# Projections on four column groups of TensorE in place of the whole array, in a two-layer attention kernel

## The chip, the cores and the metric

The kernel runs on one core of a Trainium2 chip. The metric is the device time of one execution in microseconds (us); the median of several runs is quoted, with the lowest and highest in brackets. The work is bound by TensorE, the matrix engine, an array of 128 rows (the contracted dimension, partitions of the two inputs) by 128 columns (partitions of the output). A matmul can use the whole array (written 128\*128 below), four groups of 32 rows (32\*128, four small contractions side by side) or four groups of 32 columns (128\*32, four narrow outputs side by side).

A **wave** below is four matmuls, one for each group, that run at once. A **pass** is one matmul record of the trace: a matmul of f32 stands there as two records, so as two passes. A **set** is the four matmuls that take the place of one full-width matmul, so two waves. A **hand-over** is the distance between the start of the last matmul of one shape and the first of the next.

## The reference

Eight images of 32 x 32 positions and 512 channels go through two layers; each adds an attention over the group-normalised input. Cut to what matters:

```
# layer 0: 16 heads of 32 channels, N = 1024 positions
qkv = gn(x) @ w_qkv                          # 3 projections 512 -> 512
attn = softmax(q * 32**-0.5 @ k^T)           # per head, 1024 x 1024
x = x + (attn @ v) @ w_proj + b_proj         # 1 projection

# layer 1: 4 heads of 128 channels, with relative position logits
q, k, v = gn(x) @ Wq, gn(x) @ Wk, gn(x) @ Wv # 3 projections
scores = q @ k + position_logits(q)          # small matmuls with pos_emb_w, pos_emb_h
x = x + (softmax(scores) @ v) @ Wo           # 1 projection
```

That is eight projections an image, everything in f32.

## The kernel before

The first attention is a chain of 64 steps an image. A step has scores in four row groups, `exp` on ScalarE (ACT), and the product with v in four column groups. Its sums of `exp` are made by VectorE (DVE) and finished by a small matmul in four column groups:

```python
# attention_0, front: scores, 32*128
for r in range(HB):                       # HB = 4
    nc.tensor.matmul(ps[:, r, :], k[m][rows, j*P:(j+1)*P], q[m][rows, h*NB:(h+1)*NB], start=True, stop=True)
nc.scalar.activation(e, ps, AF.Exp, scale=D0 ** -0.5)    # ps has one buffer
# back: product with v, 128*32
    nc.tensor.matmul(acc[r*D0:(r+1)*D0, :], v[:, j, c0:c0+D0], e[:, r, :], start=(j == 0), stop=(j == NT-1))
nc.vector.tensor_add(state["esum"], state["esum"], e)
# finish, after eight steps: su = sum of esum, 128*32; then reciprocal on VectorE
```

`ps` has one buffer, so the next scores can't start before `exp` has read the last ones. Into the time in which TensorE would wait for `exp`, the kernel weaves the other work of the neighbouring images, above all the projections. There are three helpers, all with the same loop; a bank of PSUM gets four matmuls over the contracted chunks `cc`, so eight passes:

```python
def project_T(xn, w, dsts, name):
    for m in range(CC):
        for h in range(NH):
            pa = bank(f"pa_{name}_{m}_{h}")
            for cc in range(CC):                  # CC = 4
                nc.tensor.matmul(pa, w[:, cc, m*P:(m+1)*P], xn[cc][:, h*NB:(h+1)*NB],
                                 start=(cc == 0), stop=(cc == CC - 1))
            evacuate(dsts(m)[:, h*NB:(h+1)*NB], pa)       # copy on ScalarE
            yield CC
# project_rows and product_T: the same loop
```

The argument will come to the position logits as well. Their matmuls are in column groups of 32, and each result is written as a rounded number by ScalarE and a rest by VectorE, one needing the other:

```python
nc.scalar.copy(view[rows], pp[rows, :, i])                                      # "posT", ACT CAST
nc.vector.tensor_sub(view[rests], pp[rows, :, i], view[rows].bitcast(F32))      # "posT", DVE
```

## Time and profile before

| | before |
|---|---|
| median of 3 runs | 4286.79 us (4285.86 to 4296.93) |
| profiled execution, span | 4285.4 us |
| TensorE (PE) busy | 97% |
| VectorE, ScalarE busy | 54%, 39% |
| idle of TensorE ahead of the first attention's scores | 49.6 us, of which 49.2 ended by `exp` |
| share of TensorE in the chain that ended last | 85% |

Busy time is the union of an engine's instructions over the span. An engine at 97% that also carries the chain is the bound: what is taken off it comes off the time, unless what comes next was waiting for another engine. The lines are shown and read in the prediction.

### The profile page before, as it was taken

What the parts mean: (1) busy time and instruction counts of PE and PEld (TensorE: products, weight loads), DVE (VectorE), ACT (ScalarE), POOL (GpSimd) and SP (SyncE); (2) the same over time, 40 slices, a digit from 0 to 9 for tenths busy, and PEclk for the clock granted to TensorE, in tenths of its full rate; (3) what the DMA queues carried; (4) which work ended last, traced back from release to release, by engine and by line L of the source; (5) the groups of instructions that cost most, each with busy time, mean ns of one, the idle gap of its engine ahead of it and who ended that gap; (6) DMA issues with size and microseconds to landing.
All of it is one profiled execution on the core that took longest, in us unless ns stands there. A gap on an engine that the chain in (4) does not pass through costs nothing.

```text
span 4285.4 us, 42293 instructions
## 1 busy us (share of the span) xinstructions
PE 4167.0 (97%) x17602; PEld 1577.6 (37%) x17602; DVE 2313.8 (54%) x2105; ACT 1673.2 (39%) x1793; POOL 247.9 (6%) x155
## 2 busy tenths in 40 slices
PE   7999999999999999999999999999999999999998
PEld 3222333333333333333333333333333333333443
DVE  2565466354663547635576355663556635467334
ACT  1553444324443244432444324443244333444131
POOL 0000000000010000100000000000000000000000
PEclk9999999999999999999999999999999999999999
DMA  4101110131101311012110121102210022010201
GB/s 118 35 20 45 30 40 1 40 89 30 40 1 40 89 30 40 1 54 74 33 37 1 69 59 42 28 1 74 58 41 15 1 74 55 30 40 1 84 15 21
DMA packets 320808, 170.66 MB, mean 40 GB/s; under 512 B 271424, under 2 KB 271456, under 8 KB 320608
## 3 DMA queue, kind: packets, MB, share of 16 engines
q1 hardware_dynamic: 320512, 167.81, 13.7%
q8 instruction: 140, 2.29, 0.2%
q14 instruction: 60, 0.49, 0.0%
q0 software_dynamic: 96, 0.07, 0.0%
HBM read 117.51 MB, written 50.33 MB: 39 GB/s over the span
## 4 chain that ended last, share of the span: by engine, by line
PE 85%; DVE 8%; ACT 4%; issue 1%; DMA 0%; POOL 0%; SPq 0%; DVEq 0%; ACTq 0%; POOLq 0%
PE ps L270 11%; PE pa_q L208 11%; PE pp L456 10%; PE ps L379 10%; PE acc L289 10%; PE pa_v L223 10%; PE acc L391 9%; PE pa_k L208 7%; DVE rc L256 3%; PE ps L380 2%; ACT e L278 2%; DVE posT L366 2%; DVE es L300 2%; ACT posT L365 2%; PE su L309 1%
## 5 line engine op out<-in xcount | busy, mean ns | idle before, releaser
L300 DVE TENSOR_TENSOR es<-es,e 128x2048 f32<-128x2048 f32 x384 | 889.5, 2316 | 919.2 <-ACT e L278 918.9
L278 ACT ACTIVATE e<-ps 128x2048 f32<-128x2048 f32 x512 | 961.7, 1878 | 838.1 <-PE ps L270 724.1
L270 PE MATMUL ps<-q,k 32*128 32x512 f32 x4096 | 609.5, 644 | 49.6 <-ACT e L278 49.2
L256 DVE RECIPROCAL rc<-su 128x512 f32<-128x512 f32 x128 | 429.3, 3355 | 316.4 <-PE su L309 297.6
L379 PE MATMUL ps<-q,k 128*128 128x512 f32 x1024 | 547.6, 616 | 14.9 <-DVE checks L237 14.3
L289 PE MATMUL acc<-e,v 128*32 128x512 f32 x4096 | 553.2, 611 | 1.0 <-ACT e L278 1.0
L391 PE MATMUL acc<-e,v 128*128 128x512 f32 x1024 | 525.4, 596 | 0.7 <-ACT e L382 0.7
L382 ACT ACTIVATE e<-ps 128x512 f32<-128x512 f32 x512 | 305.1, 597 | 563.5 <-PE ps L380 455.5
L258 POOL TENSOR_TENSOR q<-hd,rc 128x512 f32<-128x512 f32 x128 | 225.8, 1764 | 3506.2 <-DVE rc L256 3288.0
L380 PE MATMUL ps<-posT,sel 128*128 128x512 f32 x512 | 406.9, 795 | 0.0
L402 DVE TENSOR_TENSOR es<-es,e 128x512 f32<-128x512 f32 x384 | 277.0, 721 | 162.6 <-ACT e L382 151.8
L270 PEld LDWEIGHTS ps<-q,k 32*128 32x128 f32 x4096 | 166.3, 184 | 422.1 <-issue 205.7
L379 PEld LDWEIGHTS ps<-q,k 128*128 128x128 f32 x1024 | 174.9, 189 | 338.0 <-issue 259.0
L391 PEld LDWEIGHTS acc<-e,v 128*128 128x128 f32 x1024 | 192.9, 190 | 151.3 <-issue 110.9
L128 ACT COPY q<-pa_q 128x512 f32<-128x512 f32 x128 | 74.9, 585 | 440.1 <-PE pa_q L208 439.8
L208 PE MATMUL pa_q<-x0T,wq 128*128 128x512 f32 x512 | 236.9, 609 | 5.3 <-DMA wq<-in_L_conv_w_qkv 4.6
L223 PE MATMUL pa_v<-wv,x1T 128*128 128x512 f32 x512 | 236.7, 612 | 2.3 <-DVE posT L366 2.3
L366 DVE TENSOR_TENSOR posT<-pp,posT 32x256 fp32r<-32x256 f32 x256 | 130.2, 509 | 196.6 <-ACT posT L365 195.1
L208 PE MATMUL pa_q<-x1T,wq 128*128 128x512 f32 x512 | 232.9, 606 | 3.1 <-DVE x1T L192 3.1
L208 PE MATMUL pa_k<-x0T,wk 128*128 128x512 f32 x512 | 233.7, 602 | 0.0
L223 PE MATMUL pa_v<-wv,x0T 128*128 128x512 f32 x512 | 233.3, 602 | 0.0
L208 PE MATMUL pa_k<-x1T,wk 128*128 128x512 f32 x512 | 232.4, 602 | 0.6
(67 smaller groups left out, 2822.4 us busy)
## 6 DMA issues: line engine op xcount, KB each, us to landing
xs<-in_x SPq DMA_DIRECT2D x128, 128.0 KB, 3.1
d<-x0T SPq DMA_DIRECT2D x32, 512.0 KB, 3.7
x1T<-d SPq DMA_DIRECT2D x32, 512.0 KB, 5.9
d<-x1T SPq DMA_DIRECT2D x32, 512.0 KB, 2.6
x2T<-d SPq DMA_DIRECT2D x32, 512.0 KB, 6.7
out<-ot SPq DMA_DIRECT2D x256, 64.0 KB, 1.9
wq<-in_L_conv_w_qkv SPq DMA_DIRECT2D x8, 1024.0 KB, 7.7
wk<-in_L_conv_w_qkv SPq DMA_DIRECT2D x8, 1024.0 KB, 6.0
```

The source lines that it names most:

```text
L208: nc.tensor.matmul(pa, w[:, cc, m * P : (m + 1) * P], xn[cc][:, h * NB : (h + 1) * NB], start=(cc == 0), stop=(cc == CC - 1),)
L223: nc.tensor.matmul(pa, xn[cc][:, t * P : (t + 1) * P], w[:, cc, :], start=(cc == 0), stop=(cc == CC - 1),)
L256: nc.vector.reciprocal(rec, su)
L270: nc.tensor.matmul(ps[:, r, :], k[m][rows, j * P : (j + 1) * P], q[m][rows, h * NB : (h + 1) * NB], start=True, stop=True,)
L278: nc.scalar.activation(e, ps, AF.Exp, scale=D0 ** -0.5)
L289: nc.tensor.matmul(acc[r * D0 : (r + 1) * D0, :], v[:, j, c0 : c0 + D0], e[:, r, :], start=(j == 0), stop=(j == NT - 1),)
L300: nc.vector.tensor_add(state["esum"], state["esum"], e)
L379: nc.tensor.matmul(ps, k[h][:, keys], q[:, h, queries], start=True, stop=False)
L380: nc.tensor.matmul(ps, sel[:, keys], posT[h][:, queries], start=False, stop=True)
L382: nc.scalar.activation(e, ps, AF.Exp, scale=1.0 / math.sqrt(D1))
L391: nc.tensor.matmul(acc, v[:, j, h * D1 : (h + 1) * D1], e, start=(j == 0), stop=(j == NT - 1),)
L456: nc.tensor.matmul(pa, w[:, cc, m * P : (m + 1) * P], y(cc)[:, h * NB : (h + 1) * NB], start=(cc == 0), stop=(cc == CC - 1),)
```

## The change

The intent: the product with v already runs in four column groups of 32. If the projections run in the same shape, TensorE goes from one to the other without changing shape. The program also holds a general path, which it takes only if its check of the sums of `exp` fails; it is unchanged, and the quick path alone is edited. There the three projection helpers call a new one:

```diff
+    def by_columns(out, weights, moving, start, stop):
+        for g in range(P // 32):
+            columns = slice(32 * g, 32 * g + 32)
+            nc.tensor.matmul(
+                out[columns, :], weights[:, columns], moving, start=start, stop=stop
+            )
 ...
             for cc in range(CC):
-                nc.tensor.matmul(
+                by_columns(
                     pa,
                     w[:, cc, m * P : (m + 1) * P],
                     xn[cc][:, h * NB : (h + 1) * NB],
 ... (the same edit in project_rows and product_T)
```

Each full-width matmul becomes four of 32 columns with the same moving operand. Line numbers in the profile are 8 higher after the change.

More of the change, by code (lines that the diff above doesn't have):

```diff
@@ L222, in project_rows @@
             for cc in range(CC):
-                nc.tensor.matmul(
+                by_columns(
                     pa,
@@ L455, in product_T @@
         for cc in range(CC):
-            nc.tensor.matmul(
+            by_columns(
                 pa,
```

## The prediction

> **What bounds the kernel now.** I read the page's busy shares and the chain that ended last, then the groups, then the timeline of TensorE in stretches small enough to see its hand-overs.
>
> ```profile
> PE 4167.0 (97%) x17602; PEld 1577.6 (37%) x17602; DVE 2313.8 (54%) x2105; ACT 1673.2 (39%) x1793; POOL 247.9 (6%) x155
> ...
> PE 85%; DVE 8%; ACT 4%; issue 1%; DMA 0%; POOL 0%; SPq 0%; DVEq 0%; ACTq 0%; POOLq 0%
> ...
> L270 PE MATMUL ps<-q,k 32*128 32x512 f32 x4096 | 609.5, 644 | 49.6 <-ACT e L278 49.2
> L289 PE MATMUL acc<-e,v 128*32 128x512 f32 x4096 | 553.2, 611 | 1.0 <-ACT e L278 1.0
> L208 PE MATMUL pa_q<-x0T,wq 128*128 128x512 f32 x512 | 236.9, 609 | 5.3 <-DMA wq<-in_L_conv_w_qkv 4.6
> L223 PE MATMUL pa_v<-wv,x0T 128*128 128x512 f32 x512 | 233.3, 602 | 0.0
> ```
>
> TensorE is busy 97% and is 85% of the chain, so a microsecond taken off TensorE is worth nearly a microsecond. The groups name the shape of the array: 32*128 (four row groups) for the first attention's scores, 128*32 (four column groups) for its product with v, 128*128 for the projections. A projection makes 32 matmuls of f32; eight batches of it are 256, and the group says x512: each f32 matmul stands as two records, two passes. There are eight projections a batch, so 8 x 512 = 4096 records, which this change makes 16384.
>
> The pace of a full-width projection is read where nothing else runs:
>
> ```profile
> 82.37 27.63 PE L223 MATMUL pa_v<-wv,x0T 128*128 128x512 f32 x64
> 109.93 1.14 PE L270 MATMUL ps<-q,k 32*128 32x512 f32 x8
> ```
>
> (109.93 - 82.37) / 64 = 0.431 us a pass, hand-over at the end included; in the records of single matmuls the distance is 0.429 us, in 3367 of some 3390 cases. The mean of 602 to 609 ns in the group is a latency: it overlaps the next pass.
>
> A stretch in the steady state, where a step of the first attention is followed by a sum and a projection:
>
> ```profile
> 438.53 1.14 PE L270 MATMUL ps<-q,k 32*128 32x512 f32 x8
> 439.60 1.07 PE L289 MATMUL acc<-e,v 128*32 128x512 f32 x8
> 440.48 1.04 PE L309 MATMUL su<-es,ones 128*32 128x512 f32 x8
> 441.45 3.70 PE L208 MATMUL pa_q<-x1T,wq 128*128 128x512 f32 x8
> 445.08 1.14 PE L270 MATMUL ps<-q,k 32*128 32x512 f32 x8
> ```
>
> Start to start: scores 1.07, product 0.88, sum 0.97, projection 3.63 us. Eight matmuls in four groups are two waves, 2 x 0.429 = 0.858; the projection is 8 x 0.429 = 3.432. What is over is 0.21, 0.02, 0.11 and 0.20. The only hand-over that costs next to nothing is the one from 128*32 to 128*32. And this shows the pace of column groups: the second wave of the product and both of the sum start 0.429 us apart, four matmuls at once in each, the same as one full-width pass.
>
> The weight loads tell the rest:
>
> ```profile
> 438.52 0.31 PEld L270 LDWEIGHTS ps<-q,k 32*128 32x128 f32 x8 [0.76 <-issue]
> 439.60 0.16 PEld L289 LDWEIGHTS acc<-e,v 128*32 128x32 f32 x8 [0.76 <-ACT q L128]
> 440.05 0.13 PEld L309 LDWEIGHTS su<-es,ones 128*32 128x32 f32 x4 [0.30 <-issue]
> 440.48 0.13 PEld L309 LDWEIGHTS su<-es,ones 128*32 128x32 f32 x4 [0.30 <-issue]
> 441.45 0.30 PEld L208 LDWEIGHTS pa_q<-x1T,wq 128*128 128x128 f32 x2 [0.84 <-issue]
> ```
>
> The sum's loads start at 440.05, behind the product's last wave. The projection's first load starts at 441.45, with its matmul, not ahead of it: across a change of shape nothing is loaded ahead. So a change costs twice, once for emptying the array (records: 522 ns instead of 429 between the last and the first start) and once for the first load not hidden: the first pass of a full-width block lasts 533 ns to the second instead of 429, that of a column block 453.
>
> **What the Trainium skill says.** "TensorEngine Tiling (Array Packing)", section Key Properties: a change of tiling mode drains TensorE, a change of tile does not. The trace agrees: 93 ns more. "TensorE: Matmul & The Clock Gate", section Measured speedup vs the span model: tiles start about 4 ns apart and run together. Here they start 7 ns apart, 20 ns from first to fourth. The same page, LDWEIGHTS (loading the stationary operand), gives columns / 1.2 ns, 27 ns for 32 and 107 for 128; the trace has 106 to 110 and 181 to 190, so the trace's are used. The same page, Step-by-step, step 2, gives some 62 ns of decoding a MATMUL where it is done in software; four a wave leave 107 ns each.
>
> **The change part by part.** Arithmetic, moving data and results are the same; each full-width pass of 0.429 us becomes a wave of four column matmuls of 0.429 us. In itself that gains nothing: the work is not small in either direction, so no idle part of the array is filled. Added are 12,288 matmul records and as many loads. What moves are the hand-overs. I sorted the matmul records by start and counted neighbours, by shape:
>
> - Column block to projection: 333, of which 312 at the plain 522 ns (542 from the last wave's first matmul). Each now costs 542 + 533 for the first two passes; as one shape 2 x 429. Saved 217 ns: 312 x 0.217 = 67.7 us.
> - Projection to column block: 45, 43 plain, 32 of them into the position logits (pp). 522 + 453 becomes 858: 117 ns x 43 = 5.0 us.
> - Projection to scores (row groups): 287. The change of shape stays, and must now wait for the fourth group, 20 ns later: -5.7 us.
> - Projection to a full-width block (second attention, group norm): 21, now free, then 217 ns: -4.6 us. The other way round: 9 x 117 ns = -1.1 us.
> - Scores to projection: 7, with 80 ns less first load: +0.6 us.
>
> Sum 61.9 us. Not all of it arrives. In the first batch's stage (113 to 360 us, when there are only projections to fill the gaps) some 15 of 64 steps take 3.1 us and are held by the chain of scores 1.07, exp 1.88 and the next scores; 15 x 0.2 = 3 us don't count. And there, projections were taken in pieces, half a bank at a time: the instruction order made when the program is built may now cut between the four groups of a set, and a cut set costs two waves more, 0.858 us. I put 5 us for that, a guess. Left: 54 us, 1.3%.
>
> **The rivals.**
>
> 1. *The wave is slower than 0.429 us when it lasts.* The trace has at most four waves in a row; a solo projection is 64. Per wave there are eight instructions in 429 ns, 54 ns each. For it: over 50 us TensorE never took more than one per 59 ns so far. Against it: the position logits start 64 matmuls and 64 loads from 459.91 to 461.80 us, 15 ns each, and the densest 20 us have 445 instructions, 45 ns each. If the rate were 62 ns an instruction, a wave would be 0.496 us and 4096 of them 274 us longer: 4560 us. If four streams of the same tile disturbed each other in memory, it would be similar; but the product with v already reads four streams from 128 partitions at 0.429 us.
> 2. *Cut sets.* If the order breaks most of the first stage's 96 sets (24 banks by 4), up to 50 x 0.858 = 43 us are lost and the gain is 15 us: 4270 us.
> 3. *Something else takes over.* DVE 54% and ACT 39% are far from it, and a step with a whole projection has 5.5 us or more against the 3.1 us of scores and exp. The gain should arrive.
> 4. *It is much faster,* as four groups on small work would be. For it speaks only the intent; L289's 4096 records in 553.2 us against L379's 1024 in 547.6 show equal array time for equal work.
>
> **Range and chances.** 4286.8 - 54 gives 4232 us. Without losses it would be 4225; with some unforeseen gain 4210; with cut sets 4270 and a little more for a wave that is some ns slower: 4285. Faster by 2% needs 4201 us, more than all the countable hand-overs: 0.05. Slower by 2% needs 21 ns a wave or more on top: 0.08.
>
> **What would show it.** Right: waves 0.429 us apart in the solo projection before 110 us, which still takes 27.5 us; the hand-over product to projection without the 0.11 us; the projection's loads ahead of it, behind the product's last wave; projection to scores still some 0.11 us; twelve thousand more matmuls but nearly the same busy TensorE. Wrong: waves over 440 ns apart, groups of a set started in different steps, or new idle time of TensorE ended by exp or by the DVE.

## The result, and the profile after

The changed kernel took **4242.48 us** (4241.89 to 4243.49, 4 runs) against 4286.32 us (4283.82 to 4296.93, 4 runs) for the kernel before on the same chip. The ratio is 0.9893, 95% interval 0.9876 to 0.991. Ratios here are the mean time of one kernel's fast runs over that of the other's in the same rounds, so they are not quite the ratio of the quoted medians. The outputs are correct. The profiled executions took 4285.4 us before and 4239.9 us after, 45.5 us apart; all accounts by place below are of these two.

The page of the changed kernel, busy times, chain and TensorE groups (the columns of a group: line, engine, operation, output and inputs, shape, count, then busy us and mean ns, then idle time ahead and what ended it):

```profile
PE 4111.0 (97%) x29890; PEld 1367.7 (32%) x29890; DVE 2314.6 (55%) x2105; ACT 1673.7 (39%) x1793; POOL 248.7 (6%) x155
...
PE 85%; DVE 8%; ACT 4%; issue 1%; DMA 0%; POOL 0%; SPq 0%; DVEq 0%; ACTq 0%; POOLq 0%
...
L278 PE MATMUL ps<-q,k 32*128 32x512 f32 x4096 | 610.1, 645 | 58.4 <-ACT e L286 58.2
...
L297 PE MATMUL acc<-e,v 128*32 128x512 f32 x4096 | 553.3, 611 | 1.0 <-ACT e L286 1.0
...
L206 PE MATMUL pa_q<-x0T,wq 128*32 128x512 f32 x2048 | 237.0, 600 | 5.4 <-DMA wq<-in_L_conv_w_qkv 4.7
```

TensorE has 12,288 more instructions, as counted beforehand, yet is busy 56 us less (4167.0 before); the share in the chain hasn't moved. A projection group is four times as many records in the same busy time (237.0 us; 236.9 before). One number has grown that nothing in the plan should have made grow: the idle time ahead of the scores, 49.6 us before, is 58.4 us.

TensorE's timeline of the changed kernel, start and length in us, at the end of the projections that run alone and at the same steady step that the prediction shows of before:

```profile
82.41 27.65 PE L206 MATMUL pa_v<-wv,x0T 128*32 128x512 f32 x256
110.00 1.14 PE L278 MATMUL ps<-q,k 32*128 32x512 f32 x8
...
437.12 1.07 PE L297 MATMUL acc<-e,v 128*32 128x512 f32 x8
438.00 1.04 PE L317 MATMUL su<-es,ones 128*32 128x512 f32 x8
438.86 3.62 PE L206 MATMUL pa_q<-x1T,wq 128*32 128x512 f32 x32
442.41 1.14 PE L278 MATMUL ps<-q,k 32*128 32x512 f32 x8
```

Alone: (110.00 - 82.41) / 64 = 0.431 us a wave, hand-over included, exactly as a full-width pass before; in the records, waves start 0.429 us apart. Four column groups with the same moving operand are neither faster nor slower than the whole array. In the steady step, sum to projection is 0.86 us in place of 0.97, and projection to scores is 3.55 us in place of 3.63. The weight loads of the same kernel at this place show why:

```profile
438.00 0.13 PEld L317 LDWEIGHTS su<-es,ones 128*32 128x32 f32 x4 [0.30 <-issue]
438.43 0.13 PEld L206 LDWEIGHTS pa_q<-x1T,wq 128*32 128x32 f32 x4 [0.30 <-issue]
```

The projection's first load is at 438.43, a wave ahead of its matmul at 438.86, where before it came with the matmul.

I sorted the matmul records by start and put the distance between neighbours into classes by shape. A distance over 640 ns is split into a plain 520 ns and a wait. Then the account of the 45.5 us is:

| between neighbours | before | after | difference |
|---|---|---|---|
| column block to projection, plain | 172.8 us (333) | 137.4 us (340) | -35.4 |
| within projections, plain | 1644.5 us | 1625.5 us | -19.0 |
| projection to column block, plain | 23.5 us (45) | 19.6 us (51) | -3.9 |
| projection to full width and back, plain | 13.2 us (32) | 16.1 us (32) | +2.9 |
| all others, plain | | | +2.8 |
| waits | 115.3 us | 122.9 us | +7.6 |

The plain parts sum to -52.6 us, and with the waits it is -45.0; the rest of the 45.5 lies ahead of the first matmul and behind the last. Of the +7.6 us of waits, +10.3 are from a projection to the next scores (35.5 to 45.8 us). In some stretches of 3.4 or 6.8 us the profile has TensorE's granted clock at 0.5, and passes of the projections start some 0.85 us apart; what they take longer counts as a wait here. These stretches, the one behind the last work left out, sum to 54.6 us before and 47.8 after. So at most some 3 us of the 45.5 come from this half clock, an estimate: half of the difference.

Where along the run it comes is just as telling. The first scores of the second image start at 361.2 us before and 361.7 us after: the first image's whole stage, from 110 us on, gained nothing. The later images gain 3 to 11 us each; part of that spread is stretches at half clock, which differ from image to image (last section).

**The first stage.** VectorE, ScalarE and TensorE in the changed kernel, a stretch in which a finished sum falls (timeline; the bracket is the idle time ahead of an instruction and what ended it):

```profile
150.34 3.36 DVE L264 RECIPROCAL rc<-su 128x512 f32<-128x512 f32 x1 [1.27 <-PE su L317]
...
154.35 2.92 DVE L306 TENSOR_TENSOR es<-e,e 128x2048 f32<-128x2048 f32 x1
...
157.36 1.88 ACT L286 ACTIVATE e<-ps 128x2048 f32<-128x2048 f32 x1 [3.25 <-DVE es L306]
...
159.29 1.14 PE L278 MATMUL ps<-q,k 32*128 32x512 f32 x8 [0.63 <-ACT e L286]
```

The same stretch before:

```profile
154.64 2.88 DVE L298 TENSOR_TENSOR es<-e,e 128x2048 f32<-128x2048 f32 x1
...
157.62 1.88 ACT L278 ACTIVATE e<-ps 128x2048 f32<-128x2048 f32 x1 [3.00 <-DVE es L298]
159.54 1.14 PE L270 MATMUL ps<-q,k 32*128 32x512 f32 x8
```

Once in eight steps `exp` has to wait for VectorE, which makes reciprocal, check and first sum one after the other (3.36 + 0.69 + 2.92 us), before a buffer for `exp` comes free. Before, TensorE was busy almost long enough to cover it: 157.62 + 1.88 = 159.50, and the scores start at 159.54. The timeline shows no wait, but the records do: 580 ns between the last start of the projection and the first of the scores, in place of 522, so a wait of 0.06 us. After, TensorE is there earlier and waits 0.63 us (1223 ns, so 0.70 us by the records). This is a wait that was almost covered before, and waits of this kind come eight times in the stage: from projections to scores they sum to 0.7 us before and 5.4 after.

The stage has a second loss. In the records, its projections stood in 54 blocks before, mostly of four passes. After, 36 of 55 blocks have four waves, but seven have 14 records, three and a half waves, and seven have only two records: the two passes of one group's matmul, cut off from its set. (A **block** is a run of projection matmuls with no others between them.) The 14 records take 1308 ns from first start to last, four whole waves take 1307: nothing is saved where the matmul was cut off, and where it stands its two passes cost 2 x 0.429 = 0.858 us, as the prediction has it for a cut set. Seven of these are 6 us; four more uneven blocks, of 10, 22, 10 and 6 records, last 16 waves where 12 would do, another 1.7 us. Altogether the blocks of the stage lasted 66.4 us before and 69.2 after, where 54 times the 0.085 us that a four-pass block has become shorter should have saved 4.6.

**The position logits.** A step of the changed kernel while they are written (timeline):

```profile
986.27 1.14 PE L278 MATMUL ps<-q,k 32*128 32x512 f32 x8
...
988.23 3.62 PE L206 MATMUL pa_k<-x1T,wk 128*32 128x512 f32 x32
...
989.79 0.36 ACT L373 CAST posT<-pp 32x256 fp32r<-32x256 f32 x1 [0.67 <-DVE posT L374]
...
990.70 0.60 ACT L373 CAST posT<-pp 32x256 fp32r<-32x256 f32 x1 [0.55 <-DVE posT L374]
991.11 1.90 ACT L286 ACTIVATE e<-ps 128x2048 f32<-128x2048 f32 x1
...
993.06 1.14 PE L278 MATMUL ps<-q,k 32*128 32x512 f32 x8 [1.22 <-ACT e L286]
```

The same step before:

```profile
995.66 1.14 PE L270 MATMUL ps<-q,k 32*128 32x512 f32 x8
...
1000.45 1.90 ACT L278 ACTIVATE e<-ps 128x2048 f32<-128x2048 f32 x1
...
1002.40 1.14 PE L270 MATMUL ps<-q,k 32*128 32x512 f32 x8 [0.97 <-ACT e L278]
```

On ScalarE the casts run ahead of `exp`, and each cast between two scores but the first waits for VectorE's subtraction. So from one scores to the next it takes 6.79 us after and 6.74 before, although TensorE has less to do in between: it now waits 1.22 us in place of 0.97. Outside the first stage, the waits from a projection to the scores were 34.9 us at 18 places before and 40.5 us at 23 places after; the five new places are one step an image, of 0.35 us each, that did not wait before.

### The profile page after: what moved, and what is told of

Its sections match the earlier page's. It is cut to its first block, busy times and chain, and to the rows that moved or that the text cites. A ratio compares the mean times of both kernels' runs of the same rounds, so it can differ in the third digit from the quotient of the medians.

```text
span 4239.9 us, 66880 instructions
## 1 busy us (share of the span) xinstructions
PE 4111.0 (97%) x29890; PEld 1367.7 (32%) x29890; DVE 2314.6 (55%) x2105; ACT 1673.7 (39%) x1793; POOL 248.7 (6%) x155
## 4 chain that ended last, share of the span: by engine, by line
PE 85%; DVE 8%; ACT 4%; issue 1%; DMA 0%; POOL 0%; SPq 0%; DVEq 0%; ACTq 0%; POOLq 0%
PE ps L278 11%; PE pa_q L206 10%; PE ps L387 10%; PE pp L206 10%; PE acc L297 10%; PE acc L399 10%; PE pa_v L206 10%; PE pa_k L206 7%; ACT e L286 3%; PE ps L388 3%; DVE rc L264 2%; DVE posT L374 2%; DVE es L308 2%; ACT posT L373 2%; PE su L317 1%
## 5 line engine op out<-in xcount | busy, mean ns | idle before, releaser
L278 PE MATMUL ps<-q,k 32*128 32x512 f32 x4096 | 610.1, 645 | 58.4 <-ACT e L286 58.2
L206 PE MATMUL pa_q<-x0T,wq 128*32 128x512 f32 x2048 | 237.0, 600 | 5.4 <-DMA wq<-in_L_conv_w_qkv 4.7
L206 PE MATMUL pa_v<-wv,x1T 128*32 128x512 f32 x2048 | 230.5, 598 | 2.9 <-DVE posT L374 2.9
L206 PE MATMUL pa_k<-x1T,wk 128*32 128x512 f32 x2048 | 231.9, 595 | 0.6
L206 PE MATMUL pa_k<-x0T,wk 128*32 128x512 f32 x2048 | 232.3, 592 | 0.0
L206 PE MATMUL pa_v<-wv,x0T 128*32 128x512 f32 x2048 | 231.6, 592 | 0.0
L206 PE MATMUL pa_q<-x1T,wq 128*32 128x512 f32 x2048 | 228.3, 595 | 3.1 <-DVE x1T L192 3.1
```

The source lines that it names most:

```text
L206: nc.tensor.matmul(out[columns, :], weights[:, columns], moving, start=start, stop=stop)
L278: nc.tensor.matmul(ps[:, r, :], k[m][rows, j * P : (j + 1) * P], q[m][rows, h * NB : (h + 1) * NB], start=True, stop=True,)
```

## The experiments

My theory, A: the gain is the hand-overs and loads between equal shapes and nothing else, and it was partly swallowed in the first stage and at the position logits. Rivals, B: the gain comes from something else that narrow matmuls bring (smaller loads, four streams), or what is missing was lost by the waves themselves. All kernels but two gave correct results; those two are wrong on purpose. Runs are in the fast state unless said otherwise; kernels were measured against the kernel before on the same chip.

### Two groups of 64 columns: is it the shape?

```diff
-        for g in range(P // 32):
-            columns = slice(32 * g, 32 * g + 32)
+        for g in range(P // 64):
+            columns = slice(64 * g, 64 * g + 64)
```

> The changed kernel, with two groups of 64 columns in place of four of 32. Theory A (what was gained is the change of shape between the product with v, 128*32, and the projection; 128*64 is another shape): the 522 ns hand-over comes back, only the first load not hidden is shorter (some 50 ns against 104), so 0.05 us at some 330 places: 4262 to 4280 us, near the kernel before. Theory B (what was gained comes from several groups running at once, or from shorter loads): 4242 to 4252 us, near the changed kernel.

Measured: 4284.19 us (4281.27 to 4287.76, 14 runs) against 4289.7 (4276 to 4298.61, 19 runs), ratio 0.999 (0.998 to 0.9999). TensorE's timeline at the steady step:

```profile
444.05 1.04 PE L317 MATMUL su<-es,ones 128*32 128x512 f32 x8
445.02 3.65 PE L206 MATMUL pa_q<-x1T,wq 128*64 128x512 f32 x16
```

The 0.97 us between sum and projection are back, and 522 ns at 314 of 334 hand-overs. Column groups as such bring nothing: they have to be the groups of the neighbour. What little is gained is the narrower first load: 480 ns from first to second pass of a block in place of 533, so 51 ns over 429 in place of 104. The time is 4 us above the range that theory A gave it; in this kernel, too, sets are cut in the first stage, which took 5.0 us longer than before.

### Every other set whole: what does a change of shape cost?

```diff
+    turn = [0]
     def by_columns(out, weights, moving, start, stop):
+        turn[0] ^= 1
+        if turn[0]:
+            nc.tensor.matmul(out, weights, moving, start=start, stop=stop)
+            return
```

> The changed kernel, with every other set of a projection full-width again, so that full-width and column passes alternate within each bank: no pass is longer, but four changes of shape stand in each of 512 banks. Theory A (each change into full width costs 217 ns, each into columns 117 ns, wherever it is): 512 x 2 x (217 + 117) = 342 us more than without any, less the 72 us of the kernel before that are contained in it: 4551 us, 4520 to 4575. Theory B (the cost belongs to the hand-over between attention and projection, not to the shape): between the two kernels, 4240 to 4290 us.

Measured: 4528.48 us (4523.34 to 4529.51, 4 runs), ratio 1.0555 (1.0529 to 1.0582), so 239 us more than before. TensorE's timeline while only projections run:

```profile
60.36 1.07 PE L212 MATMUL pa_q<-x0T,wq 128*32 128x512 f32 x8
...
62.41 1.07 PE L212 MATMUL pa_k<-x0T,wk 128*32 128x512 f32 x8
```

Two whole passes and two waves now take 62.41 - 60.36 = 2.05 us; of one shape they take 4 x 0.429 = 1.716. The pair of changes costs 0.334 us, which is 117 + 217 ns, the two sizes that the prediction took from the hand-overs. In the whole run the account of neighbours has the plain parts 270.9 us longer than before, and theory A asks for 342 - 72 = 270. The waits are 28.7 us shorter (14.6 of them from projections to scores), part of it because the clock was halved for 30.7 us in place of 54.6; hence the 22 us less than the middle of the expectation.

### The first stage whole: did it gain anything?

```diff
+    whole = [False]
     def by_columns(out, weights, moving, start, stop):
+        if whole[0]:
+            nc.tensor.matmul(out, weights, moving, start=start, stop=stop)
+            return
 ...
     def before_0(b, st):                  # whole only for the projections of the second image,
+        whole[0] = b == 1                 # which fill the first image's stage
```

> The changed kernel, with the projections of the second batch, which fill the first batch's attention, full-width as before. Theory A (in that stage the hand-overs saved go into a wait for exp, itself held by VectorE's reciprocal and sum, and into sets cut between steps, so the stage gained nothing): 4242 us within 3. Theory B (the stage gained its 48 x 0.2 us like every other, and the rest of the missing gain is elsewhere): 4251 us or more.

Measured: 4242.53 us (4240.78 to 4244.31, 6 runs), ratio 0.9892 (0.9874 to 0.9911), the same as the change (0.9893). The stage ends at 361.2 us in the kernel before and in this one (here it began 1.4 us earlier and ran at half clock for 3.4 us longer). Making that stage's projections in columns or whole is worth nothing: its hand-overs are shorter, and all of it is lost again.

### A short chain on VectorE in the first stage, in both kernels: how much is the wait?

In batch 0's first attention, a copy takes the place of the reciprocal (0.69 us in place of 3.36). The results are wrong on purpose. The same edit in the kernel before and in the changed one:

```diff
-        nc.vector.reciprocal(rec, su)
+        (nc.vector.tensor_copy if cheap else nc.vector.reciprocal)(rec, su)   # cheap: batch 0
```

> The kernel before, with a copy in place of the reciprocal in the first batch's first attention alone (its result is wrong on purpose): VectorE's chain sum, reciprocal, addition, exp is some 2.8 us shorter for every eight steps. To be compared in the first stage with the next run. Expected: eight steps there take 29.0 to 30.0 us in place of 30.7, bound by TensorE.

> The changed kernel with the same copy. Theory A (the chain held the stage, and one cut set is left): eight steps of the first stage take 0.4 to 1.0 us less than in the run before this one, where with the reciprocal both took 30.7. Theory B (what holds the stage is not that chain): no difference between the two.

Measured, one run each (state unknown, so only the profiles are used): 4292.31 us and 4240.34 us. Eight steps of the stage took 30.7 us in both kernels without the edit. With it they take 30.6 us in the kernel before, where I had expected 29 to 30: a miss, and it says that TensorE, not VectorE, bound the kernel before there, but for some 0.1 us. In the changed kernel they take 30.0 us. Its scores at the place shown above come without the wait (timeline of the changed kernel with the copy):

```profile
159.53 1.14 PE L278 MATMUL ps<-q,k 32*128 32x512 f32 x8
```

Over the whole stage the changed kernel gains 4.0 us on the other (250.6 and 246.6 us). So the 0.63 us waits are real and the chain of VectorE makes them. They are some 4 us of the stage's 10. The other 7 us are what the cut sets leave by the account above; no kernel without cuts was run, so this part is counted in records, not shown by an experiment.

### Casts on VectorE, on top of the change: does the queue ahead of `exp` hold the rest?

```diff
-                    nc.scalar.copy(view[rows], pp[rows, :, i])
+                    nc.vector.tensor_copy(view[rows], pp[rows, :, i])
```

ScalarE then has `exp` and plain copies, and nothing that waits for VectorE in turn.

> The changed kernel, with the copies of the position logits out of PSUM on VectorE in place of ScalarE. Theory A (in that stage ScalarE does the copies in turn with VectorE, exp stands behind them and scores wait: 40 us of waits ahead of scores after projections in all, against 35 before the change): most of these waits go, 4205 to 4225 us, and the hand-overs saved there arrive. Theory B (VectorE then becomes what is waited for, as its sums and the copies stand in one queue): 4235 to 4270 us.

Measured: **4188.08 us** (4187.0 to 4191.53, 5 runs), ratio 0.9766 (0.9745 to 0.9787): faster than both kernels. TensorE's instructions stand in the same order as in the changed kernel. From its page:

```profile
PE 4096.0 (98%) x29890; PEld 1364.7 (33%) x29890; DVE 2444.0 (58%) x2361; ACT 1558.1 (37%) x1537; POOL 248.6 (6%) x155
...
L278 PE MATMUL ps<-q,k 32*128 32x512 f32 x4096 | 608.3, 643 | 25.3 <-ACT e L286 25.1
```

The idle time ahead of the scores is 25.3 us in place of 58.4, and from a projection to the scores it is 11.2 us in place of 45.8. The gain, 54 us, is more than I expected: I had not thought that the casts held up so much. Not all of it is the queue itself. TensorE's clock was halved for 27.3 us in this run and for 47.8 us in the changed kernel's, so up to 10 us of the gain, an estimate from half of the difference, came by way of the clock: fewer long waits, fewer stretches at half clock.

### Casts alone, in the kernel before: how much of the change do the waits swallow?

The same edit in the kernel before.

> The kernel before, full-width projections, with the copies of the position logits on VectorE: the other corner of the square. Theory A (some 8 of the 62 us of hand-overs were swallowed by the waits for exp in that stage, and come through once those waits are gone): 52 us, within 4, slower than the kernel with both, which had 4188: 4236 to 4244 us. Theory B (the two gains simply add): 44 us slower, 4229 to 4235 us.

Measured: 4244.06 us (4240.37 to 4245.83, 5 runs) against 4285.19 (4282.17 to 4299.05, 9 runs), ratio 0.9899 (0.9884 to 0.9913). Its page has 21.0 us of idle time ahead of the scores:

```profile
L270 PE MATMUL ps<-q,k 32*128 32x512 f32 x4096 | 607.5, 643 | 21.0 <-ACT e L278 20.7
```

The four kernels' profiled executions side by side:

| span, us | casts on ScalarE | casts on VectorE |
|---|---|---|
| whole projections | 4285.4 | 4238.6 |
| projections in columns | 4239.9 | 4187.1 |

The change is worth 45.5 us with the casts on ScalarE and 51.5 us with them on VectorE. The change adds 58.4 - 49.6 = 8.8 us of idle time ahead of the scores with the one and 25.3 - 21.0 = 4.3 us with the other, and the latter is about the first stage's. So some 5 us of the shorter hand-overs went into waiting at the position logits, and this waiting is gone when the queue ahead of `exp` is short. The times alone would not settle so small a difference: the two kernels of the second column ran on different chips, and the quotient of their ratios, 0.9766 / 0.9899 = 0.987, differs from the change's 0.9893 by no more than the intervals of these ratios leave open. It is the idle times that carry it; TensorE's clock was halved for 27.3 us in both kernels of the second column, so that part doesn't differ there.

### All of one group, then the next: does the order of a set matter?

The loops over `cc` and over the group are exchanged, so that a bank gets its eight passes of group 0, then of group 1, and so on:

```diff
         for g in range(P // 32):
             columns = slice(32 * g, 32 * g + 32)
-            nc.tensor.matmul(out[columns, :], weights[:, columns], moving, start=start, stop=stop)
+            for cc in range(CC):
+                nc.tensor.matmul(out[columns, :], weights(cc)[:, columns], moving(cc),
+                                 start=(cc == 0), stop=(cc == CC - 1))
```

> The changed kernel with the two loops of a bank exchanged: all four sets of column group 0, then of group 1, and so on; the same matmuls in another order. Theory A (TensorE finds the next group's passes far enough ahead of the one it works on to keep four groups busy): 4240 to 4262 us. Theory B (it sees only a few instructions ahead, so a group's eight passes run before the next group's begin): up to 4096 x 3 x 0.429 = 5270 us more; anything over 4600 us speaks for it.

Measured: 6500.09 us (6499.39 to 6502.4, 4 runs), ratio 1.516 (1.5135 to 1.5186). Where only projections run, 256 matmuls take 57.2 us in place of 27.5: two groups run at once, not four. TensorE's timeline, where one projection ends and the next begins:

```profile
139.26 0.62 PE L207 MATMUL pa_v<-wv,x0T 128*32 128x512 f32 x1
139.68 0.59 PE L207 MATMUL pa_k<-x0T,wk 128*32 128x512 f32 x1
139.71 0.59 PE L207 MATMUL pa_v<-wv,x0T 128*32 128x512 f32 x1
140.11 0.59 PE L207 MATMUL pa_k<-x0T,wk 128*32 128x512 f32 x1
```

In the program all of `pa_k` stands ahead of all of `pa_v`. On the chip, a matmul of `pa_v` starts while `pa_k` still has three passes to go, which start later: matmuls of different groups do not start in program order. They only look a little ahead. The trace doesn't name the groups, but the program begins a bank with group 0, and the records fit this: in 232 of the 247 blocks of one or two banks the first four starts are 429 ns apart, one at a time, and then two come together, some 1716 and 1722 ns after the first: the fifth pass of group 0 and, as I read it, the first of group 1.

### Two sets by group: how far ahead?

Group 0 gets two sets (four passes), then groups 1, 2, 3 get theirs; then the next two sets.

```diff
+        for c0 in range(0, CC, 2):
             for g in range(P // 32):
                 columns = slice(32 * g, 32 * g + 32)
+                for cc in (c0, c0 + 1):
                     ...
```

> Between the changed kernel and the run with the groups outermost: two sets of group 0, then of group 1, 2 and 3, then the next two sets. Theory A (a pass may start past at most three earlier passes that have not started yet, which fits the run with the groups outermost: 20 waves for a bank of 8, 36 for two banks): stepping this rule through gives 11 waves for a bank in place of 8, 19 for two, so three waves or 1.29 us more in each of some 300 blocks: 4600 to 4660 us. With a rule of four, 10 waves: 4490 to 4530; of two, 14 waves: over 4900. Theory B (a group may look past any number as long as its own queue has room, and the groups outermost were slow for another reason): 4242 to 4260 us.

Measured: 4265.62 us (4263.96 to 4266.99, 4 runs) against 4288.37 (4283.26 to 4300.2, 7 runs), ratio 0.9944 (0.9925 to 0.9963). I had made a rule after the last run (a matmul starts only if at most three earlier ones have not); it asked for 4600 us and more and has fallen. All four groups start within some 33 ns at the head of a block here. The rule that fits both runs: passes are handed out in program order to four queues, one for each column group, and each holds four passes, one running and three waiting. A fifth pass of one group then stops the handing out. With eight passes a group, a bank of eight waves should take 12 + 8 = 20 waves and two should take 36; from the first start to the last the records have 8.24 and 15.23 us, 19.2 and 35.5 times 0.429, where 20 and 36 waves have 19 and 35 distances. With four, nothing is held up at first. I made this rule from these two runs and haven't tested it on a third. The 23 us over the change itself are not explained by it as it stands: a block of eight waves takes 3078 ns from first to last start in place of 3024. Its last wave begins after 3004 ns in both, but its four matmuls start over 73 ns in place of 20: the later groups fall behind. Why they do is open.

### What could not be tried

The second attention in columns too would do away with the last changes of shape on that side. It doesn't compile with its fp32r matmul in column groups. A third buffer for `exp` would take away the first stage's wait. It doesn't fit into SBUF. Both were built only and never ran.

## Why the prediction was right

4232 us was predicted and 4242.48 measured: inside the range, within 2% of before as the 0.87 (what 0.05 and 0.08 leave) had it, and 10 us from the middle. By its steps:

- **Pace.** A wave is 0.429 us, as predicted, also when 256 matmuls run alone; the first rival, a slower wave, is out.
- **Hand-overs.** Column block to projection fell from 522 ns (at 312 of 333 places) to 409 ns from the fourth group's start (at 310 of 340), which is 429 from the first. Projection to scores stayed at 522, counted from the fourth group, as the prediction had it. The exchange of sets (the second experiment) gives the sum of the two sizes, 117 and 217 ns, again: 0.334 us for the pair.
- **Loads ahead.** They stand a wave ahead of the matmul, as predicted. With 64 columns, which is another shape, they don't.
- **Sum of the hand-overs.** 61.9 us predicted; 52.6 us counted net. Most of the 9.3 us between them is the first stage, where the plain parts fell by 3.2 us and not by some 10, for the cut sets (7 us). The costs came as predicted: 21 full-width blocks behind a projection lost 2.0 us in the hand-over and, with 104 ns each in the first load, 2.2 us inside the block (in the table's "all others"), 4.2 us where 4.6 were expected.
- **Losses.** This is the step that was mis-sized: "Left: 54 us" allowed 8 us, and 61.9 - 45.0 = 17 us were lost, some 11 of them in the first stage and 5.6 at the position logits. In the first stage it was the whole gain, some 10 us (54 blocks at 0.113 in the hand-over and 0.085 in the block), where 3 + 5 were allowed. Cut sets were named, and that the 5 us for them, called a guess, came near the 7 counted is partly luck. The wait for `exp` was named too, but for other steps: those of 3.1 us (17, where it says 15), and in the steps without a projection the wait didn't grow, it fell from 9.7 to 8.6 us. What came was 0.6 to 0.7 us once in eight steps, behind the reciprocal; I had not read that `exp` already ended last there, with nothing to spare.
- **The third rival was dismissed too easily.** "A step with a whole projection has 5.5 us or more against the 3.1 us of scores and exp" counts ScalarE as if it were free when the scores end. At the position logits, `exp` stands behind casts that wait for VectorE, and the step shown lasts 6.7 us before and 6.8 after. The 49.6 us of idle time ahead of the scores, in the line that the prediction itself quotes, were the sign: I took them as given, and didn't ask what delays `exp` there. This cost 5.6 us here. What the casts cost altogether is 41 us in the kernel before and 54 in the changed one, as the cast experiments show, half-clock time included.

## What to carry to other kernels

Splitting a full matmul into column groups gained nothing in itself here; it gained what the change of shape to its neighbours cost, so count the hand-overs, in both directions, and look whether the shapes are exactly the same. Keep a set of four together in the program: one group after the other within each set (4242 us), not all sets of one group before the next group (6500 us). And see that what weaves instructions together doesn't cut it. When an engine at 97% still has idle time ahead of one group, look at what stands in the queue ahead of the instruction that ends it: here one word, the engine of a cast, was worth as much as the whole change, and the two together are 2.3% faster than the kernel before.

## What the Trainium skill lacked or had wrong

- "TensorE: Matmul & The Clock Gate", section The mechanism (Part 3), says that MATMULs are "pc-monotone in start AND end". With column groups they are not: matmuls of the next projection started at 139.26 us, ahead of earlier ones in the program at 139.68, 140.11 and 140.54. No page says how far the array looks ahead in each group, though it decides between 4242 and 6500 us for the same matmuls; two runs fit four passes a group.
- The same page, section LDWEIGHTS (loading the stationary operand), gives columns / 1.2 ns, which is 27, 53 and 107 ns for 32, 64 and 128 columns. In f32 the traces have 106 to 110, 133 to 137 and 181 to 190 ns: some 80 ns more each.
- "TensorEngine Tiling (Array Packing)", section Key Properties, says that a change of mode drains TensorE, which all runs confirm, but gives no size. Here it is 93 ns of emptying (522 in place of 429) and the first load that can't be hidden, 24, 51 and 104 ns for 32, 64 and 128 columns. 128\*64 and 128\*32 count as different modes (522 ns at 314 of 334 places).
- No page says what column groups do to a matmul that fills the array: nothing, 0.429 us a wave against 0.429 us a pass.
- In a kernel that is 97% busy, TensorE still drops to half its clock for 3.4 or 6.8 us, 12 times before and 13 times after (without the end, when its work is done), following waits of its own. The first of the two pages, in its Part 1, has the half clock come after at least one idle window of some 3.4 us. Here less is enough: in the kernel before, the clock was halved from 1749.6 us on, and in the 3.4 us ahead of that TensorE waited once, for 1.26 us, and was busy for 2.14. One wait of 3.16 us, which five images have alike, came with 3.4 us of half clock in three of them and with 6.8 in two; these five had 3.4 or 10.2 us of it in all and took 527.5 to 530.9 us.
